# Splitting the first layer's filter copies by rounds, and drawing out the other layers' copies, in a four-layer convolution kernel

## The chip, the core and the metric

The kernel runs on one core of a Trainium2 chip. A core has five engines with queues of their own: TensorE (PE, with its weight loads PEld), VectorE (DVE), ScalarE (ACT), GpSimd (POOL) and SyncE (SP), which in this kernel issues the DMAs. Sixteen DMA engines move the data. The metric is the device time of one execution in microseconds (us); several executions are made and their median is taken.

## The reference

Four layers work on x of shape (4, 64, 256, 256), that is batch, channel, row, column. Layers 0, 2 and 3 are long two-dimensional convolutions, each with its own weights; layer 1 works in Haar space.

```python
h = sin(freq * (z @ w1 + b1)); h = sin(freq * (h @ w2 + b2)); h = sin(freq * (h @ w3 + b3))
h = (h @ wo) * exp(-t * abs(deltas))          # once for X, once for Y: hx, hy
k = einsum('ijk,imk->ijmk', hx, hy)           # a filter per channel, an outer product
y = irfft2(rfft2(x) * rfft2(k) / fft_size)[..., :L, :L]
out = y + x * bias                            # layers 0, 2, 3

f1 = haar2d(x)                                # layer 1
for i in range(2):
    f4 = einsum('bchw,oc->bohw', f1 * v[i], conv_w[i])
    acc += sign(f4) * relu(abs(f4) - tau[i])
out = haar2d(acc, inverse=True) + x
```

The filter of a channel is an outer product of two causal filters of 256 taps, so a convolution layer is two products with triangular Toeplitz matrices, one along each image axis. The small network that makes the taps is the same function for the three convolution layers ("first": layer 0; "other layers": 2 and 3, which the kernel counts as 1 and 2).

## The kernel before

The work is cut into three phases. Phase A does layer 0 and the forward Haar transform, phase B the channel mixing of layer 1, phase C the inverse Haar transform and layers 2 and 3. The images are two groups of two, and a round is two channels of one group: 32 rounds a group, 64 in phase A.

**A round of phase A** is ten pieces (`A_PIECES`), functions called one after another; `piece(t, j)` is piece j of round t, at place 10t + j. In pieces 0 to 3 TensorE multiplies round t's rows by the first Toeplitz blocks (`rows`, tile a1ps); in pieces 4 and 5 it does the Haar product of round t-3 (`product`, a3ps); in pieces 6 to 9 it does the columns of round t-1 (`columns`, a2ps). ACT copies a1ps out (L444), DVE adds the residual (`residual`, L464) and scales a3ps (L477), POOL does the rest of the Haar transform of round t-2 (L344, L346). The copies and residuals of a piece are issued at the start of the next piece (`later`, `flush`). All DMAs of the phase are issued by SP, in the order of the program: `filters(t + 2)` in piece 2 (two loads of overlapping rows from DRAM, L158), `store(t - 3)` in piece 7 (coef, L481), `load(t + 2)` in piece 9 (x, four loads in the first group, L147). The x tiles are three, so a load waits until the last residual that reads its buffer is done.

**The filters.** `network(ls)` gives a list of small functions for the networks of layers `ls`: for each of three depths a product on TensorE (L193, L195), a shift and six steps of a range reduction on DVE (L200 to L215), and a sine on ACT (L219); at the end, for each layer, three output products (L236), each with a multiplication by the decay on DVE (L241). The result stands in a tile `padded` of 64 rows (partitions): two for each round, each with three items of 320 elements. A Toeplitz load reads 64 shifted rows, so the taps have to stand repeated in DRAM, 20 times (`REPEATS`), in `filt`. `spread(l, begin, end, parts)` (L258) writes these repetitions for the rounds `begin` to `end`, as `parts` DMAs: each takes the partitions 2 begin to 2 end, reads them with a step of 0 over its share of the 20 repetitions, and writes 3840 bytes for each row and repetition (L264). The filters of the first four rounds (`FIRST`) are made in another way, by a product that gives the repetitions at once (`repeated`, L227), before phase A begins.

The copies of the remaining 28 rounds of layer 0 are `spread(0, FIRST, ROUNDS, BLOCKS)`: four DMAs of 56 rows by 5 repetitions, issued in pieces 0 to 3 of round 0.

**What is set beside phase A.** The list `rest` (L282 to L285) holds a load of weights for the other layers (`wbd`), the 39 functions of `network([1, 2])` and the 20 copies of the two other layers, ten each, of 64 rows by 2 repetitions: 60 entries. `beside(main, side, lead, tail)` (L949) calls the pieces of `main` and after each as many entries of `side` as keep the two lists in step, spread evenly from piece `lead` to `tail` pieces before the end. The call `beside(a[:cut_a], rest, 2, 3 * A_PIECES)` has 348 pieces with 2 and 30 left out, so 60 entries over 316 pieces: one in every 5.27. After `cut_a`, in round 34, the network's tiles are given back and phase B begins beside the second group's rounds.

The pieces' part that the change touches:

```python
            if t == 0 and j < BLOCKS:
                copies[j]()
            if j == 2:
                filters(t + 2)
...
        copies = spread(0, FIRST, ROUNDS, BLOCKS)
```

## Time and profile before

| What | Before |
|---|---|
| Median of 3 runs | 2587.52 us (2584.11 to 2591.82) |
| The profiled execution | 2585.35 us, span 2583.6 us |
| Mean granted TensorE clock | 0.977 |
| Busy: TensorE, weight loads | 2319.3 us (90%), 1848.1 us (72%) |
| Busy: VectorE, ScalarE, GpSimd | 1823.0 us (71%), 1324.7 us (51%), 2064.4 us (80%) |
| DMA | 685.23 MB, mean 265 GB/s |
| `filt` copies of layer 0 | 4 of 1050 KB, issued from 26.6 to 35.1 us |
| `filt` copies of the other layers | 20 of 480 KB, issued from 274.5 to 387.5 us |
| `toep` loads, whole kernel | 384 of 224 KB, median 5.3 us from issue to landing |

The span runs from the first to the last instruction; the execution's time has a little around it. Shares of busy time are means over phases of different kinds. Phase A alone runs from about 24 us to 425 us, and from there beside phase B. The profile can also be asked for a window, for one engine's instructions in order of time, or for one engine's waits; a line such as "x<-in_x x4" is four instructions in a row that write tile x from the input of that name, with the start of the first and the time of all. "SPq" is the issuing of DMAs, which says nothing of how long their data take. A bracket behind an instruction gives the idle time of its engine before it and what ended that.

### The profile page before, as it was taken

The page shows a single profiled execution, that of the slowest core. Times are in us where ns is not written, and L with a number is a line of the kernel's source. Part 1 is how long each engine was busy: PE and PEld are TensorE (multiplying, and loading weights), DVE is VectorE, ACT ScalarE, POOL GpSimd, SP SyncE. Part 2 cuts the span into 40 slices and gives each one's busy share as a digit, 9 for nine tenths or more (in the row PEclk, how much of TensorE's full clock was granted, in tenths as well). Part 3 has the DMA queues.
Part 4 walks back from the last instruction along what each step waited for, and adds up shares of the span by engine and source line. Part 5 has one row for each costly group of instructions (what it writes and reads, how often), then busy time and mean ns, then how long its engine had stood idle before and what let it go on. Part 6 is the DMA issues. An engine that isn't in the chain of part 4 may idle for free.

```text
span 2583.6 us, 118458 instructions
## 1 busy us (share of the span) xinstructions
PE 2319.3 (90%) x53292; PEld 1848.1 (72%) x53292; DVE 1823.0 (71%) x2049; ACT 1324.7 (51%) x2187; POOL 2064.4 (80%) x2428
## 2 busy tenths in 40 slices
PE   5999999678888888757999999999989999999999
PEld 4877877444444444546777778777789998999998
DVE  2555445799999999646677777766757777777763
ACT  1221212566666666325666666666655655655552
POOL 1898887899989999767676777766779999999991
PEclk8999999899999999978999999999999999999999
DMA  7676998699999999555988999988876666666653
GB/s 210 216 244 234 298 309 283 243 342 323 337 340 316 351 321 330 182 194 194 331 301 309 317 320 323 313 306 297 288 233 211 223 213 212 221 216 208 219 166 111
DMA packets 203676, 685.23 MB, mean 265 GB/s; under 512 B 29289, under 2 KB 30826, under 8 KB 190755
## 3 DMA queue, kind: packets, MB, share of 16 engines
q1 hardware_dynamic: 203171, 677.67, 77.1%
q8 instruction: 418, 6.85, 1.1%
q14 instruction: 87, 0.71, 0.1%
HBM read 427.93 MB, written 249.63 MB: 262 GB/s over the span
## 4 chain that ended last, share of the span: by engine, by line
PE 60%; DVE 14%; POOL 10%; DMA 6%; issue 5%; ACT 3%; SPq 2%; DVEq 0%; ACTq 0%; POOLq 0%
PE c2c L296 11%; PE c2r L296 10%; PE c1r L296 9%; PE c1c L296 9%; PE a1ps L296 6%; PE a2ps L296 6%; PE f L607 4%; PE c0ps L308 4%; POOL fw L344 3%; DVE m L651 3%; POOL f L346 3%; DVE x L626 3%; DVE a L646 2%; PE a3ps L308 2%; DVE x L464 2%
## 5 line engine op out<-in xcount | busy, mean ns | idle before, releaser
L385 POOL TENSOR_TENSOR i<-i,g 128x16 f32<-128x16 f32 x744 | 431.5, 601 | 27.7 <-ACT g L362 0.6
L296 PEld LDWEIGHTS a2ps<-toep,ay 64*64 64x64 f32 x8192 | 305.5, 137 | 163.9 <-DVE f L477 86.4
L296 PE MATMUL a2ps<-toep,ay 64*64 64x128 f32 (+3 forms) x8192 | 357.7, 306 | 47.9 <-DVE f L477 42.3
L607 PE MATMUL f<-ft,mix 64*64 64x512 f32 x2048 | 297.3, 617 | 111.6 <-DVE x L626 94.3
L296 PEld LDWEIGHTS a1ps<-toep,x 64*64 64x64 f32 x8192 | 288.4, 134 | 89.7 <-issue 45.4
L296 PE MATMUL a1ps<-toep,x 64*64 64x64 f32 (+3 forms) x8192 | 337.6, 300 | 16.6 <-DMA x<-in_x 11.4
L296 PEld LDWEIGHTS c2c<-toep,ch 64*64 64x64 f32 x8192 | 300.0, 135 | 58.9 <-issue 19.1
L296 PE MATMUL c1r<-toep,z 64*64 64x192 f32 (+3 forms) x8192 | 319.0, 300 | 22.6 <-issue 11.9
L296 PEld LDWEIGHTS c1c<-toep,ch 64*64 64x64 f32 x8192 | 296.2, 134 | 57.8 <-issue 18.5
L296 PEld LDWEIGHTS c1r<-toep,z 64*64 64x64 f32 x8192 | 292.4, 135 | 59.2 <-issue 28.0
L296 PE MATMUL c2c<-toep,ch 64*64 64x256 f32 (+3 forms) x8192 | 314.7, 299 | 8.4 <-ACT ch L848 6.8
L296 PE MATMUL c1c<-toep,ch 64*64 64x128 f32 (+3 forms) x8192 | 310.3, 298 | 9.0 <-ACT ch L848 5.5
L669 POOL TENSOR_TENSOR gt<-m,ft 128x512 f32<-128x512 f32 x128 | 163.5, 1277 | 193.7 <-DVE m L651 188.8
L385 POOL TENSOR_TENSOR ci<-i,g 128x1024 f32<-128x1024 f32 x124 | 313.9, 2552 | 4.5
L444 ACT COPY ay<-a1ps 128x512 f32<-128x512 f32 x256 | 137.4, 589 | 351.2 <-PE a1ps L296 350.6
L296 PEld LDWEIGHTS c2r<-toep,cy 64*64 64x64 f32 x8192 | 287.9, 134 | 32.9 <-issue 15.2
L632 ACT ACTIVATE m<-x 128x1024 f32<-128x1024 f32 x194 | 206.1, 1062 | 205.3 <-DVE x L626 98.5
L296 PE MATMUL c2r<-toep,cy 64*64 64x192 f32 (+3 forms) x8192 | 310.1, 297 | 1.3 <-issue 1.1
L848 ACT COPY ch<-c2r 128x512 f32<-128x512 f32 x256 | 137.3, 591 | 280.2 <-PE c2r L296 279.5
L477 DVE TENSOR_TENSOR f<-a3ps,wrow_sb 128x512 f32<-128x512 f32 x256 | 161.3, 683 | 130.2 <-PE a3ps L308 130.2
L626 DVE TENSOR_TENSOR x<-f,v 128x1024 f32<-128x1024 f32 x192 | 233.5, 1216 | 22.1 <-PE f L607 20.5
L344 POOL TENSOR_TENSOR fw<-x 128x1024 f32<-128x1024 f32 x64 | 122.2, 1910 | 150.4 <-DVE x L464 137.9
(83 smaller groups left out, 3976.8 us busy)
## 6 DMA issues: line engine op xcount, KB each, us to landing
toep<-filt SPq DMA_DIRECT2D x384, 224.0 KB, 5.3
ft<-coef SPq DMA_DIRECT2D x128, 512.0 KB, 7.6
v<-in_v SPq DMA_DIRECT2D x64, 1024.0 KB, 10.1
mixed<-gt SPq DMA_DIRECT2D x128, 512.0 KB, 7.2
g<-mixed SPq DMA_DIRECT2D x256, 256.0 KB, 5.1
x<-in_x SPq DMA_DIRECT2D x128, 256.0 KB, 4.4
coef<-f SPq DMA_DIRECT2D x128, 256.0 KB, 4.0
x<-in_x SPq DMA_DIRECT2D x32, 1024.0 KB, 8.0
```

What stands on the lines that cost most here:

```text
L296: nc.tensor.matmul(ps[r][half(c), j % 2, k * ROW :], data[half(r), c, k, bass.ts(j, ROW)], t(r, c)[:, : N - k * ROW], start=k == 0, stop=k ...
L308: nc.tensor.matmul(ps[r][half(c)].rearrange("p h k -> p (h k)"), matrix[half(r)], pairs(r, c).rearrange("p h k -> p (h k)"), start=True, s ...
L344: nc.gpsimd.tensor_tensor(diffs, even, odd, ALU.subtract)
L346: nc.gpsimd.tensor_tensor(sums, even, odd, ALU.add)
L385: engine.tensor_tensor(to, s, d, op)
L444: later(lambda y=y, ps=ps: nc.scalar.copy(y, ps))
L477: later(lambda f=f, ps=ps, w=w: nc.vector.tensor_tensor(f, ps, w, ALU.mult))
L607: nc.tensor.matmul(un[u]["f4"][half(q), b, :], mixers[0][half(r), bass.ts(i, C)], st[s]["f"][half(r), b], start=True, stop=True, tile_posi ...
L626: nc.vector.tensor_tensor(un[u]["x"], un[u]["f4"], both(u, "v"), ALU.mult)
L632: nc.scalar.activation(un[u]["m"], un[u]["x"], AF.Sign)
L669: nc.gpsimd.tensor_tensor(g[:, 0], m[:, 0], st[s]["f"][:, 0], ALU.add)
L848: later(lambda y=y, ps=ps: nc.scalar.copy(y, ps))
```

## The change

The four copies of layer 0 become seven, one for every four rounds (`CHUNK`), each with all 20 repetitions of 8 rows, 600 KB. The dictionary `copies` says in which round one is issued: the one for rounds 4 to 7 in round 0, the one for 8 to 11 in round 2, and so on every fourth round (6, 10, 14, 18, 22), six rounds ahead of its first use, always in piece 1, ahead of the Toeplitz load in piece 2.

The list `rest` is drawn out with empty entries: one ahead of each function of the networks, and nine ahead of each copy (`APART` - 1). It has 1 + 78 + 200 = 279 entries over the same 316 pieces, one in 1.13. So a network function comes in every 2.27 pieces, from round 0 to round 9, where it came in every 5.27, from round 1 to round 21; and a copy of the other layers comes in every 11.3 pieces, from round 10 to round 31, where it came in every 5.27, from round 21 to round 31. Data, sizes of the other layers' copies and all arithmetic stay as they are.

```diff
 FIRST = 4
+CHUNK = 4
+APART = 10
...
     rest = []
     rest.append(lambda: wbd_sb.extend(constant(f"wbd{l}", wbd[:, l], [P, 2, P]) for l in (1, 2)))
-    rest += network([1, 2])
-    rest += spread(1, 0, ROUNDS, 10) + spread(2, 0, ROUNDS, 10)
+    for p in network([1, 2]):
+        rest += [lambda: None, p]
+    for copy in spread(1, 0, ROUNDS, 10) + spread(2, 0, ROUNDS, 10):
+        rest += [lambda: None] * (APART - 1) + [copy]
...
-            if t == 0 and j < BLOCKS:
-                copies[j]()
+            if j == 1 and t in copies:
+                copies[t]()
...
-        copies = spread(0, FIRST, ROUNDS, BLOCKS)
+        copies = {max(0, t - 6): spread(0, t, t + CHUNK, 1)[0] for t in range(FIRST, ROUNDS, CHUNK)}
```

## The prediction

> **What bounds the kernel now.** I read the table of busy time by stage first, because the page's averages hide where the edit acts. Its columns are the stage, each engine's busy time, the granted TensorE clock, the DMA share and GB/s.

> ```profile
> core 0: us, PE busy (x) PEld busy (x) DVE busy (x) ACT busy (x) POOL busy (x), PEclk, DMA share, GB/s
> 0.00:40.00 40.00, 23.79 (x348) 15.98 (x349) 13.55 (x33) 6.83 (x12) 1.47 (x8) 1.00 0.74 199
> 40.00:80.00 40.00, 26.96 (x583) 25.12 (x586) 10.43 (x18) 4.30 (x8) 17.87 (x25) 0.79 0.66 191
> 120.00:160.00 40.00, 40.00 (x1044) 31.85 (x1040) 23.84 (x37) 8.05 (x15) 36.19 (x63) 1.00 0.69 233
> 280.00:320.00 40.00, 39.85 (x1031) 32.72 (x1027) 21.19 (x32) 7.24 (x15) 35.78 (x64) 1.00 0.97 317
> 360.00:400.00 40.00, 36.20 (x920) 30.66 (x915) 18.46 (x29) 6.44 (x12) 30.34 (x55) 1.00 0.91 298
> ```

> From 80 to 310 us TensorE is full and the DMA engines are idle a quarter of the time. It has holes at the start (0 to 80) and once the DMA share is above 0.9. Next the chain of waits (start, duration, what):

> ```profile
> 123.38 4.37 PE a1ps L296 x128
> 133.83 4.37 PE a1ps L296 x128
> ...
> 306.66 4.42 PE a1ps L296 x109
> 339.43 4.78 PE a1ps L296 x90
> 389.76 4.52 PE a1ps L296 x115
> ```

> The first two lines are one full round, 10.45 us. Round 25 starts at 306.66, round 28 at 339.43, round 32 at 389.76: from 28 to 32 a round takes 12.6 us. From round 24 (first matmul at 296.03) to round 34 (411.40), ten rounds take 115.4 us where full ones take 104.5: 10.9 us lost. Then SP's queue, start and duration of issue:

> ```profile
> 24.61 1.87 SPq L147 DMA_DIRECT2D x<-in_x  x4
> 26.58 3.13 SPq L264 DMA_DIRECT2D filt<-padded  x3
> 29.76 5.29 SPq L158 DMA_DIRECT2D toep<-filt  x2
> 35.09 2.59 SPq L264 DMA_DIRECT2D filt<-padded  x1
> 37.72 5.55 SPq L169 DMA_DIRECT2D wbd_sb<-in_wbd  x2
> 43.32 8.38 SPq L147 DMA_DIRECT2D x<-in_x  x4
> ...
> 81.77 2.50 SPq L147 DMA_DIRECT2D x<-in_x  x4
> 84.78 1.20 SPq L158 DMA_DIRECT2D toep<-filt  x2
> 86.88 3.64 SPq L481 DMA_DIRECT2D coef<-f  x4
> ```

> and TensorE's own timeline:

> ```profile
> 42.87 4.07 PE L296 MATMUL a2ps<-toep,ay 64*64 64x256 f32 x60 [3.22 <-issue]
> 56.57 1.08 PE L296 MATMUL a1ps<-toep,x 64*64 64x256 f32 x2 [9.63 <-DMA x<-in_x]
> 58.19 7.18 PE L296 MATMUL a1ps<-toep,x 64*64 64x256 f32 x118 [0.54 <-DMA x<-in_x]
> ```

> The four first-filter copies hold back the load of x_2, and round 2 waits for it until 58. In a full round (79.92) the x load for the next one goes out 1.85 us in, when the residual frees its buffer, the Toeplitz load at 4.9, the store at 7.

> [...] each 56-row copy (partitions 8 to 63) landed in 14 single increments, each 64-row copy in 16. [...] a 3840-byte packet of the 64-row copies takes 149 ns alone and 293 ns in the crowd[...]. The coef stores, 64 rows too but every second partition, take 159 ns for 4096 bytes on the same 16 engines, so the halving belongs to partitions, not to engines. [...] x_2, issued behind the copies, came when they had landed (34.98, 40.94, 47.06, 53.27: 6.1 us each). [...] Above, 118 matmuls took 7.18 us after a 9.63 us hole; 128 take 4.37 in a full round.

> **The change part by part.**

> *The first filters' copies.* Four DMAs of 56 rows x 5 repeats become seven of 8 rows x 20 repeats, 614 KB each, in piece 1 of rounds 0, 2, 6, 10, 14, 18, 22. The bytes are the same (4.3 MB). [...] By the two-engine figure a packet is 2 x 293 = 586 ns, so 20 take 11.7 us (estimate[...]). The seven take 82 us against 24.5 now, on engines that carry everything else.

> Startup: x_1 has left the engines at 29.4, where the first copy packet starts now. The copy ends at 41.1; the Toeplitz load adds 1.5, the wbd weights (256 KB) 0.7, x_2 3.3, the landing 1.2: 47.8 against 58.2. Of these 10 us I keep 9 at round 4, since the second copy (begun about 53, ended 65) leaves x_4 behind it: 65 + 1.5 + 2.7 + 1.2 = 70.4 against 79.9 now. **9 us won.**

> The copy of round 6, in a full stage, round start T. SP passes x_7 at T+1.85 to 4.3, then the copy, two Toeplitz loads, four coef stores, and x_8's four parts from T+12.3. Engines 0 to 7: x_7 done at 5.5, copy until 17.2, Toeplitz 1.5 (18.7), coef 2.8 (21.5), x_8 3.3 (24.8), landing 1.2: T+26. SP also cycles through eight DMA semaphores in the trace, and x_8's second part is the eighth DMA behind the copy, so it is not issued before about T+18. TensorE wants x_8 at T+20.9[...]: 5 us of stall, and about 1 for the half clock. **6 us lost.** Queued behind the waiting matmul are all later rounds, so ACT's copies, DVE's residuals and POOL's transform shift with it.[...]

> Copies of rounds 10, 14, 18, 22 meet the other layers' copies (below). A round costs each engine 7.9 us of packets, a 64-row copy 1.66 us, now every 1.13 rounds: 9.4. Four rounds with a first-filter copy ask 4 x 9.4 + 11.7 = 49.3 us of engines 0 to 7, and have 41.8. The missing 7.5, with imperfect packing (the 12.6 us rounds are 0.93 busy), is 8 us a copy, from 7 to 11. **32 us lost.** The extra SP issues (three DMAs, 0.4 to 0.6 us each) lie in SP's idle time.

> *The other layers' copies.* Twenty 480 KB copies at pieces 217 to 317 (1.9 a round) move to 102 to 317 (0.88 a round). Rounds 24 to 33 then need 9.4 us of DMA in 10.45, and the stage at 285 to 306 kept full rounds with 9.95. So the 10.9 us go, less a little. **10.5 us won.**

> *The networks.* The 39 pieces go from a-pieces 12 to 212 to 5 to 91. TensorE's share is the same: two products lengthened rounds 5 and 10 by 1.4 and 1.2 us, six outputs rounds 15 to 20 by 0.7 each; 7 us, paid in either place, or up to 2 hidden in stalls. DVE's 13 us (for each of three depths two shifts of 0.5, three steps of 0.42 and three of 0.7) fall on nine rounds in place of twenty: DVE goes from 6.2 us of 10.45 (23.84 of 40 above) to about 7. A sine stands 2.3 pieces behind its last DVE step, so ACT's row copies behind it could wait 1 us, three times. I take 0 (-2 to +3). The wbd loads pass x_2's by no more than now. POOL gets nothing.

> Sum: -9 + 6 + 32 - 10.5 = +18.5. The profiled execution took 2585.35 us (span 2583.6 and 1.75 around it), 2.2 under the median of 2587.52. So 2604 by it, 2606 by the median; I give 2605. Phase B starts behind round 34 and shifts one to one.

> **Rivals.**

> *The narrow copies cost nothing* (the rival on the other side: [...]the idle quarter of the DMA time swallows the copy; it decides from a copy that holds engines 0 to 7 for less than about 4 us, with a price of 3). Then x_2 lands near 29.4 + 3 + 6.7 = 39, and round 2 starts where round 1 ends, at 46.9[...]: 58.2 - 46.9 = 11.3 plus some 3.5 of half clock, 15 us won, plus 10.5: 2560. For it: full rounds at a DMA share of 0.97. Against: 293 ns beside 149, and an x load with only about 2.5 us to spare (issued 81.8 to 84.3, median 4.1 to landing, wanted at 90.4).

> *The losses balance the gains.* The copies stall 4 us each in place of 8: -9 + 4 + 16 - 10.5 = 0.5, about 2587. For it: the 1.9 copies a round begin in round 21 and the first long round is 26, so some backlog is carried without a stall.

> [...]

> **How the numbers follow.** Forecast 0.62 (own range 2593 to 2622); free 0.20; balance 0.12[...]. A measurement here can tell 0.3%, 7.8 us. Slower by more: 0.62 + 0.06 = 0.68; same 0.12; faster 0.20. The range 2562 to 2625 leaves out half of the free case[...] and the forecast's tail.

> **What would show it.** Right: waits of TensorE for x<-in_x two rounds behind rounds 6, 10, 14, 18 and 22, of 4 to 11 us; landings of the new copies near 12 us and 3840-byte packets near 586 ns; rounds 27 to 33 at 10.45; round 3 starting near 57 to 60. Wrong: copies landing in 3 to 6 us, or full rounds through 10 to 26; then the time is near 2560.

## The result, and the profile after

The changed kernel takes 2604.05 us (median of 6 runs, 2598.79 to 2609.45) against 2583.36 us before (6 runs, 2579.76 to 2591.82): ratio 1.0077, 95% interval 1.0056 to 1.0098. It is slower by 20.7 us; the prediction said 2605, 18.5 us slower. The profiled execution took 2599.17 us with a span of 2597.4, which is 13.8 us more than the profiled span before, so it lies at the fast end of its kernel's runs. The engines' work is what it was (the matmul count is the same, 53292); the time went into holes of TensorE and into stretches behind them at half clock (a granted clock of 0.50 in the trace).

The table of busy time by stage of the kernel after, with the columns shown for before:

```profile
0.00:40.00 40.00, 25.27 (x408) 17.41 (x408) 17.08 (x39) 6.83 (x12) 1.47 (x8) 1.00 0.61 160
40.00:80.00 40.00, 35.16 (x792) 28.26 (x796) 20.71 (x30) 7.50 (x14) 28.72 (x42) 0.91 0.76 228
160.00:200.00 40.00, 37.31 (x911) 31.32 (x914) 17.29 (x26) 6.44 (x12) 29.57 (x53) 0.96 0.92 301
240.00:280.00 40.00, 34.34 (x825) 30.21 (x821) 15.91 (x25) 6.44 (x12) 28.82 (x51) 0.91 0.84 249
360.00:400.00 40.00, 40.00 (x1043) 37.89 (x1038) 19.64 (x30) 8.59 (x16) 35.46 (x62) 1.00 0.87 300
```

TensorE does 8 us more in 40 to 80 than before, and 360 to 400 is full again. In exchange the middle (160 to 320), full before, has lost 3 to 7 us in 40. A narrower window just behind the copies of rounds 6 and 14 tells what the DMA engines did there:

```profile
95.00:108.00 13.00, 13.00 (x308) 9.31 (x300) 6.90 (x11) 3.37 (x7) 12.38 (x19) 1.00 0.67 143
193.00:206.00 13.00, 10.83 (x290) 9.19 (x281) 5.29 (x8) 2.59 (x5) 11.92 (x19) 1.00 0.67 140
```

and a window of the same length in the kernel before:

```profile
134.00:147.00 13.00, 13.00 (x352) 10.41 (x347) 7.79 (x12) 2.60 (x5) 12.21 (x24) 1.00 0.68 228
```

The DMA share is the same, 0.67 and 0.68, but 140 GB/s move in place of 228: a packet counts as busy for as long as it takes, and the packets of the new copies take longer (a median of 573 ns for 3840 bytes, where the other layers' copies of 64 rows mostly show 149 or 293). SP's queue of the kernel after, around the copy of round 14 (start, duration of issue):

```profile
193.53 0.76 SPq L266 DMA_DIRECT2D filt<-padded  x1
194.39 5.89 SPq L160 DMA_DIRECT2D toep<-filt  x2
200.38 7.68 SPq L485 DMA_DIRECT2D coef<-f  x4
208.10 1.13 SPq L266 DMA_DIRECT2D filt<-padded  x1
209.33 3.82 SPq L149 DMA_DIRECT2D x<-in_x  x4
```

Behind the copy at 193.53 two Toeplitz loads take 5.9 us to issue, where they took 1.2, and four stores 7.7 where they took 3.6: SP is held back (the profile does not say by what), and x_16 goes out only at 209.33. Each of the seven copies landed in eight single increments, 14.1 to 15.4 us after its issue. Where no other copy runs beside it, seven or eight of its 160 packets are under way at once for 64 to 82% of its length, so it is called here a copy on eight engines, with 20 packets for each. Which engines they are no record says: "engines 0 to 7" is the prediction's name for them. The chain of waits near the end of the first group has its full rounds back:

```profile
362.37 4.37 PE a1ps L300 x112
372.84 4.36 PE a1ps L300 x114
```

From one to the next is a full round of 10.47 us, where the kernel before took 12.6. TensorE's timeline behind the copies of rounds 10 and 14 is a surprise:

```profile
162.11 5.38 PE L300 MATMUL a2ps<-toep,ay 64*64 64x128 f32 x105 [3.70 <-issue]
210.47 2.50 PE L300 MATMUL a1ps<-toep,x 64*64 64x64 f32 x33 [6.64 <-issue]
```

In the second line TensorE has stopped for 6.64 us in the middle of a round's rows; "issue" says that the profile shows nothing that it waits for, and x_15, which it is multiplying, had landed at 197.9. All of TensorE's own waits from 80 to 340 us in the kernel after (total, times, longest):

```profile
PE a1ps L300 <- issue: 17.0, 4, 6.6
PE a2ps L300 <- issue: 3.9, 2, 3.7
PE a1ps L300 <- DMA x<-in_x: 3.0, 4, 1.3
```

So 21 us of the holes end with no data arriving, and only 3 us with an x load. Another 15.4 us, in four stretches at the ends of the four long stops, TensorE worked at half clock (granted 0.50), where the clock before stood at 1.00 from 64 to 345 us; by the prediction's two figures, 7.18 us for 118 matmuls there (granted 0.61 over that time) and 4.37 for 128 in a full round, that costs some 7 us (an estimate).

The trace also records packets that bring instructions, 16384 bytes each, among the packets of the DMA engines. From 80 to 330 us one starts every 5.0 us (median), but not behind the copies: from 148.7 the next is 11.1 us later, from 194.6 13.4, from 243.7 12.0, from 297.9 9.9. That TensorE runs out of instructions there became the rival to test.

Counting settles much of it. The span has 418 of these packets and 107204 recorded instructions of TensorE (matmuls, weight loads and what its sequencer does), about 256 for each packet, so the packets are TensorE's. And at each of the four long stops the number of instructions that it had started is exactly 449 plus 256 for each packet that had ended by then (22, 30, 38 and 47 packets); it goes on 1.4 to 1.6 us after the next packet has ended. The two waits for x_8, at 114 and 116 us, do not stand at such places: 15 packets had ended, and TensorE had more than 180 of their instructions left. The reserve is small: when one of these packets starts, TensorE has, in 19 of 20 cases, at most 253 delivered instructions left, and a full round uses 544 in 10.45 us, so that is under 5 us of work (an estimate).

### The profile page after: what moved, and what is told of

It is laid out like the page before. It is cut to its first block, busy times and chain, and to the rows that moved or that the text cites. A ratio compares the mean times of both kernels' runs of the same rounds, so it can differ in the third digit from the quotient of the medians.

```text
span 2597.4 us, 118459 instructions
## 1 busy us (share of the span) xinstructions
PE 2330.5 (90%) x53292; PEld 1880.0 (72%) x53292; DVE 1828.5 (70%) x2049; ACT 1324.5 (51%) x2187; POOL 2064.2 (79%) x2428
## 4 chain that ended last, share of the span: by engine, by line
PE 59%; DVE 15%; POOL 8%; DMA 7%; issue 5%; ACT 4%; SPq 2%; DVEq 0%; ACTq 0%; POOLq 0%
PE c2c L300 10%; PE c2r L300 10%; PE c1r L300 9%; PE c1c L300 9%; PE a1ps L300 6%; PE a2ps L300 5%; PE f L611 4%; PE c0ps L312 4%; DMA v<-in_v 4%; DVE m L655 3%; DVE x L630 3%; POOL fw L348 2%; POOL f L350 2%; DVE a L650 2%; PE a3ps L312 2%
## 5 line engine op out<-in xcount | busy, mean ns | idle before, releaser
L300 PEld LDWEIGHTS a2ps<-toep,ay 64*64 64x64 f32 x8192 | 313.6, 138 | 154.8 <-DVE f L481 85.2
L300 PE MATMUL a1ps<-toep,x 64*64 64x128 f32 (+3 forms) x8192 | 345.0, 303 | 26.0 <-issue 17.2
L300 PEld LDWEIGHTS a1ps<-toep,x 64*64 64x64 f32 x8192 | 296.7, 136 | 98.2 <-issue 52.9
L300 PE MATMUL c1r<-toep,z 64*64 64x128 f32 (+3 forms) x8192 | 313.0, 299 | 17.5 <-ACT z L840 10.3
L300 PE MATMUL c2c<-toep,ch 64*64 64x128 f32 (+3 forms) x8192 | 309.1, 299 | 7.9 <-ACT ch L852 5.4
L300 PE MATMUL c1c<-toep,ch 64*64 64x64 f32 (+3 forms) x8192 | 308.4, 299 | 8.4 <-ACT ch L852 5.6
L300 PEld LDWEIGHTS c2r<-toep,cy 64*64 64x64 f32 x8192 | 290.6, 134 | 34.1 <-issue 21.5
L300 PE MATMUL c2r<-toep,cy 64*64 64x128 f32 (+3 forms) x8192 | 309.3, 298 | 6.3 <-issue 5.9
L481 DVE TENSOR_TENSOR f<-a3ps,wrow_sb 128x512 f32<-128x512 f32 x256 | 161.2, 683 | 147.7 <-PE a3ps L312 146.3
```

The costliest lines, as they stand in the source:

```text
L300: nc.tensor.matmul(ps[r][half(c), j % 2, k * ROW :], data[half(r), c, k, bass.ts(j, ROW)], t(r, c)[:, : N - k * ROW], start=k == 0, stop=k ...
L481: later(lambda f=f, ps=ps, w=w: nc.vector.tensor_tensor(f, ps, w, ALU.mult))
```

## The experiments

All times are compared with the kernel before on the same chip. The first two diffs are against the kernel before, the others against the changed kernel, unless another is named; only the lines that matter are shown. A profiled execution of one kernel can lie 11 us from its median, so the table after the experiments counts the delay round by round instead.

**One part alone.** First the drawn-out list without the new copies:

```diff
-    rest += network([1, 2])
-    rest += spread(1, 0, ROUNDS, 10) + spread(2, 0, ROUNDS, 10)
+    for p in network([1, 2]):
+        rest += [lambda: None, p]
+    for copy in spread(1, 0, ROUNDS, 10) + spread(2, 0, ROUNDS, 10):
+        rest += [lambda: None] * (APART - 1) + [copy]
```

> The kernel before with the drawn-out list alone (networks in every second piece, the other layers' copies one a round); the four 56-row copies of layer 0 stay in round 0. Theory (narrow reads: the loss is all in the 8-row copies, the drawn-out copies are a clean gain): the ten rounds 24 to 33 fall from 115 us to about 105, nothing is lost before, so about 10 us faster than before, 2574. Rival (the networks in nine rounds and the copies from round 10 cost as much as they bring): within 3 us of before.

Measured: 2576.35 us against 2583.5, ratio 0.9977 (0.9962 to 0.9991). Two of its stages, same columns:

```profile
280.00:320.00 40.00, 39.67 (x1057) 36.76 (x1052) 20.06 (x31) 7.51 (x14) 36.09 (x64) 1.00 0.86 282
360.00:400.00 40.00, 40.00 (x1042) 35.26 (x1037) 20.01 (x31) 8.59 (x16) 36.52 (x61) 1.00 0.84 282
```

The stages that had holes at a DMA share of 0.91 and more are full, at 0.84 to 0.86. The list is a gain by itself, 7 us by the medians where 10 were expected; the interval reaches from 2 to 10. Then the new copies without the list:

```diff
-            if t == 0 and j < BLOCKS:
-                copies[j]()
+            if j == 1 and t in copies:
+                copies[t]()
...
-        copies = spread(0, FIRST, ROUNDS, BLOCKS)
+        copies = {max(0, t - 6): spread(0, t, t + CHUNK, 1)[0] for t in range(FIRST, ROUNDS, CHUNK)}
```

> The kernel before with the seven 8-row copies alone; networks and the other layers' copies stay as before. Theory (narrow reads): start won by 11 us, then about 7 us lost behind each of the copies of rounds 6, 10, 14, 18 although no other copies run there, and 7 or more at round 22: 2583 - 11 + 35 = 2607. Rival (loss only where both kinds of copies meet): 7 us at round 6 and 7 at round 22 at most, 2583 - 11 + 14 = 2586 or less.

Measured: 2614.65 us, ratio 1.0115 (1.0098 to 1.0131), nearly 8 us over what was expected. The copies do harm alone: about 5 us behind each of the copies of rounds 10, 14 and 18, with no other copies near. TensorE's waits from 80 to 340 us here:

```profile
PE a1ps L298 <- DMA x<-in_x: 10.3, 7, 2.4
PE a1ps L298 <- DVE x L466: 3.7, 3, 1.5
PE a2ps L298 <- issue: 2.3, 1, 2.3
```

In this kernel it is mostly the x load that comes late, as predicted. Both sorts of wait occur, then.

**The rows apart.** The rows of the filter tile are put in another order, so that the eight rows of a copy stand four partitions apart. The columns of the network's last weights and of the decay are put in that order (`placed`), and the loads of the other layers find their rows in it; nothing else changes:

```diff
+def _place(row):
+    return 32 * (row // 32) + 4 * (row % 8) + row % 32 // 8
...
-            start = filt[l].offset + (t % ROUNDS * 2 + r) * REPEATS * SPAN
+            row = t % ROUNDS * 2 + r
+            start = filt[l].offset + (_place(row) if l else row) * REPEATS * SPAN
...
-            src = filters[l][at].rearrange("p k e -> p (k e)").unsqueeze(1)
+            p = _place(2 * begin)
+            of = at if l else slice(p, p + 29, 4)
+            src = filters[l][of].rearrange("p k e -> p (k e)").unsqueeze(1)
...
-        "wo": f(np.stack([w[:, filters.T] for w in wo], axis=1)),
-        "decay": f(_decay()[filters]),
+        "wo": f(np.stack([w[:, placed.T] for w in wo], axis=1)),
+        "decay": f(_decay()[placed]),
```

> The changed kernel, with the rows of the filter tile put in another order: the eight rows of a copy stand in every fourth partition (4h + c), not in eight neighbours. Same DMAs, same bytes, same places in SP's order, still eight engines. Theory[...]: [...]packets fall from 573 ns to about 149, a copy lands in 4 to 5 us, the stalls behind rounds 6 to 22 go (some 36 us less): about 2604 - 36 = 2568, 15 us under before. Rival ([...]a row read 20 times is slow): packets stay above 450 ns and the time at 2600 or more.

Measured: 2556.34 us, ratio 0.9901 (0.9874 to 0.9928), 27 us faster than before, where 15 were expected. The packets of the copies fall to a median of 149 ns, the copies land in 6.3 to 8.5 us. Its second stage, and a window behind its copy of round 6:

```profile
40.00:80.00 40.00, 40.00 (x993) 31.94 (x994) 27.25 (x39) 9.65 (x18) 35.64 (x52) 1.00 0.67 221
...
87.00:100.00 13.00, 13.00 (x304) 9.35 (x300) 6.89 (x11) 3.29 (x7) 12.37 (x19) 1.00 0.91 317
```

317 GB/s in place of 143 with the same seven DMAs of eight rows, and TensorE is full from 40 to 80 us. So in this kernel a copy of eight rows alone does little harm (149 ns a packet, 2556 us); with its rows in two groups of four neighbouring partitions it does (573 ns, 2604 us). A step between comes from every second partition, so four groups of four with two rows in each (diff against the version just shown):

```diff
-    return 32 * (row // 32) + 4 * (row % 8) + row % 32 // 8
+    return 16 * (row // 16) + 2 * (row % 8) + row % 16 // 8
...
-            of = at if l else slice(p, p + 29, 4)
+            of = at if l else slice(p, p + 15, 2)
```

> The changed kernel with the eight rows of a copy in every second partition, so over four groups of four and two engines on each. Theory[...]: packets near 293 ns, 20 of them 5.9 us, landing 8 to 10 us; little stall is left, 2556 to 2568, and not under the version with every fourth partition. Rival (it is neighbouring partitions as such, not the groups of four): packets near 149 ns or near 573 ns.

Measured: 2567.67 us, ratio 0.9937 (0.9913 to 0.9960); landings 8.6 to 9.6 us. The packets of its copies are of two sorts, most near 149 and near 293 ns (median 229 before 138 us). So in these copies of eight rows a packet took 149 ns with one row in a group of four partitions, near 149 or near 293 with two, and 573 with four, which is 2.0 and 3.8 times 149. What makes the packets of neighbouring rows slow each other is not shown beyond these times. Little stall is left: 3.7 us of waits of TensorE from 80 to 340 us.

**What the wait is.** From round 3 to 31 the x loads go into a tile that nothing reads, and TensorE multiplies the tile of round 2 instead. What this kernel leaves out is the use of those images, so its output is another:

```diff
-        xs = big("in", f"x_{t}", 3)
+        xs = spare if 2 < t < ROUNDS else big("in", f"x_{t}", 3)
...
+                if t == 2:
+                    kept.append(st[t]["x"])
+                if 2 < t < ROUNDS:
+                    st[t]["x"] = kept[0]
```

> The changed kernel, with x loaded from round 3 to 31 into a tile that nothing reads, while TensorE and the residuals read the tile of round 2 (so layer 0 is computed from the wrong images in the first group; DMA traffic is the same, but no product waits for an x load). Theory as predicted (x arrives late behind the copy): the stalls behind the copies of rounds 6 to 22 go, 2604 - 36 = 2568. Rival (TensorE's own instruction packets[...] are held up: the profile after shows gaps of 3.7 and 6.6 us that no x load ended): stalls of 4 to 7 us stay behind most of the five copies, 2590 or more.

Measured: 2598.16 us, ratio 1.0056 (1.0037 to 1.0076). TensorE's waits from 80 to 340 us:

```profile
PE a2ps L302 <- issue: 16.0, 2, 9.5
PE a1ps L302 <- issue: 7.0, 1, 7.0
PE a1ps L302 <- DMA toep<-filt: 1.6, 2, 1.1
```

With no x load to wait for, TensorE still stops for 6.5, 7.0 and 9.5 us behind the copies of rounds 6, 10 and 14. In the same places the instruction packets are 14.2, 13.2 and 15.8 us apart, and each of the three stops again stands at exactly 449 plus a multiple of 256 instructions (12, 21 and 29 packets), and ends 1.4 to 1.5 us after the next packet has ended. Behind the copies of rounds 18 and 22 no packet comes more than 7.8 us after the last, and there TensorE hardly stops. The rival is right: x late is one way to lose the time, instructions late the other, and taking the first away alone brought some 6 us (2598 for 2604). How a copy on eight engines holds an instruction packet up is not shown, since the records don't say on which DMA engine a packet ran. In the changed kernel the four late packets started between 0.1 and 5.1 us before the copy ahead of them had landed.

**Burst or amount.** Each copy is cut into four DMAs of five repetitions, one in each of four rounds (two in each of rounds 0 and 1 for the first):

```diff
+            if j == 1:
+                for put in copies.get(t, []):
+                    put()
...
-        copies = {max(0, t - 6): spread(0, t, t + CHUNK, 1)[0] for t in range(FIRST, ROUNDS, CHUNK)}
+        copies = {}
+        for first in range(FIRST, ROUNDS, CHUNK):
+            for k, put in enumerate(spread(0, first, first + CHUNK, BLOCKS)):
+                copies.setdefault(k // 2 if first == FIRST else first - 6 + k, []).append(put)
```

> The changed kernel, with each of the seven copies cut into four DMAs of 8 neighbouring rows by 5 repetitions, one in each of four rounds in a row (two and two in rounds 0 and 1 for the first). [...]a single DMA holds its engines for 5 x 573 ns = 2.9 us. Theory A (throughput: engines 0 to 7 have 9.4 + 2.9 = 12.3 us of work in a round of 10.45 from round 10 to 25): rounds 2 to 9 full, then about 30 us lost as in the changed kernel; 2583 - 14 + 30 - 10 = 2589 or more. Theory B (burst: an x load or an instruction packet stands 12 us behind one copy): short holds do no harm, 2583 - 14 - 10 = 2560 to 2566.

Measured: 2570.53 us, ratio 0.9942 (0.9923 to 0.9961), between the two but much nearer to B. The same bytes leave the same two groups of four partitions, over four rounds in place of one, and the loss is mostly gone. The packets changed with it: before 138 us their median is 154 ns in place of 573, and 20 of them take an engine 5.6 us in place of 9.5 (means). Half of them ran at 149 ns, like the packets of the rows apart; why is not shown. So this run shortens the burst and the engines' total time at once, and does not tell the two apart.

**Both together, and the list undone.** The rows apart with the other layers' list as before (the removed lines of the first diff put back):

> The seven copies with their rows in every fourth partition, and the list of the other layers as in the kernel before. Theory (parts add up): the start's 18 us stay won, rounds 24 to 33 cost their 10 us again: 2556 + 8 to 10 = 2565. Rival (the drawn-out list and the narrow copies only help one another): 2575 or more.

Measured: 2566.7 us, ratio 0.9939 (0.9915 to 0.9962). That is the 2565 expected: the parts add up. And the rows apart with the copies in quarters (the diffs of the rows apart and the burst experiment together):

> Both mendings together: rows of a copy in every fourth partition, and each copy cut into four DMAs of 5 repetitions in rounds in a row. Theory (what harms is how long one copy holds its engines): a part holds them for 5 x 149 ns = 0.75 us against 3.4 in the version with every fourth partition alone; the few us that this one loses in rounds 11 to 16 go, 2550 to 2558, not to be told from 2556. Rival (20 more DMAs on SP cost issue time and semaphores): 2565 or more.

Measured: 2558.51 us, ratio 0.9906 (0.9884 to 0.9928): not to be told from the rows apart alone (2556.34), and so no sign that the quarters bring more. Its TensorE has one sort of wait left from 80 to 340 us:

```profile
PE a1ps L303 <- issue: 1.9, 3, 1.3
```

**The delay by rounds.** The end of the last residual of a round on DVE, less that of the kernel before, in us, from each profiled execution (negative is earlier):

| Kernel | round 1 | 5 | 9 | 13 | 17 | 21 | 23 | 33 |
|---|---|---|---|---|---|---|---|---|
| after | -11.4 | -10.8 | -4.5 | 2.8 | 8.7 | 16.9 | 23.9 | 13.9 |
| list alone | -1.6 | -0.9 | 1.5 | 2.7 | -0.2 | -1.7 | -1.7 | -12.0 |
| copies alone | -12.9 | -11.0 | -7.7 | -2.6 | 2.7 | 8.0 | 17.6 | 17.5 |
| rows apart | -19.3 | -18.7 | -16.2 | -13.3 | -16.0 | -16.1 | -15.9 | -23.8 |
| x unread | -11.9 | 2.9 | 7.9 | 27.9 | 25.8 | 25.3 | 27.8 | 17.7 |
| quarters | -17.9 | -17.3 | -14.8 | -12.3 | -14.1 | -10.0 | -10.0 | -16.7 |
| every second | -18.2 | -17.5 | -15.1 | -12.7 | -14.2 | -13.5 | -12.4 | -19.0 |
| apart, old list | -19.7 | -19.7 | -19.7 | -19.7 | -19.5 | -19.5 | -19.0 | -18.4 |
| apart, quarters | -19.4 | -18.8 | -16.3 | -16.0 | -17.8 | -18.9 | -18.9 | -26.5 |

The networks stand in different rounds in the two lists, which bends the rows with the new list by up to 4 us in rounds 5 to 17 and is gone by round 21 (second line). What is there in round 33 stays to the end: the kernel after is 13.0 us behind in round 63 too.

## Why the prediction was right, and where its steps were not

*The cost of a narrow copy* (586 ns a packet, 11.7 us): right, 573 ns and eight single increments. That the 293 ns of the copies before would double was the author's estimate; the versions with one and two rows in a group have the 149 and 293 ns. The landing, 14.1 to 15.4 us after the issue, came later than the 12 given as a sign.

*The start, 9 us won*: 11.4 in round 1, of which the list has 1.6. TensorE's timeline after:

```profile
43.78 0.96 PE L300 MATMUL a1ps<-toep,x 64*64 64x256 f32 x2 [3.82 <-DMA x<-in_x]
45.80 7.03 PE L300 MATMUL a1ps<-toep,x 64*64 64x256 f32 x126 [1.07 <-DMA x<-in_x]
```

x_2 came near 46, not 47.8. The late x_4 that was to keep back part of the gain at round 4 wasn't there: the second copy was issued at 45.8, where the prediction had it begin near 53, and had landed at 59.9, so x_4 passed and round 4 began at 68.7 in place of 70.4.

*The copy of round 6, 6 us lost*: 6.3 from round 5 to 9, of which the networks' shift is 2.4 (second line of the table), so 3.9 where 6 were given. x_8 landed at 118.15, and 2.7 us of wait for it stand in the timeline: the mechanism as given, and a third of the size not there.

*The copies of rounds 10 to 22, 32 us lost*: 28.4 from round 9 to 23, where the list alone wins 3.2, so 31.6. The number is right, and its reason is the step that failed, in two ways. First, the loss was worked out as an amount: 49.3 us of work for a copy's eight engines in rounds that give 41.8. The kernel with the copies alone speaks against that. Behind its copies of rounds 10, 14 and 18 no other copies run; by the prediction's 7.9 us a round and the measured packet, four rounds there ask 4 x 7.9 + 11.5 = 43.1 us, 1.3 more than there are (with the 7.3 us a round that the packets before take from 80 to 270 us, nothing is missing), and 5.1 to 5.3 us were lost behind each. What costs, as these runs read, is the time for which one DMA is under way, 14 to 15 us from issue to landing: behind it, in the changed kernel, the instruction packets come 10 to 13 us apart in place of 5.0. (The quarters fit this, but with their 5.6 us the amount, too, gives a small loss, 4 x 9.4 + 5.6 = 43.2 against 41.8.) Second, the wait at the end was to be x: behind these four copies it was mostly TensorE's own instructions, 20.4 us of stops, a transfer that the prediction had not in its account at all. That the sum fits is in this part luck: two accounts of one blockage came to the same size.

*The other layers' copies, 10.5 us won*: 10.0 after round 23 in the changed kernel, 10.3 in the list alone. ("Idle a quarter" up to 310 us holds only until the first of these copies, at 274; the prediction's own line for 280 to 320 has a share of 0.97.) The prediction took the long rounds before for a lack of DMA time. The share is high (0.91 and more), but here too what TensorE stops for is instructions. One of four such stops, from the kernel before:

```profile
357.44 0.66 PE L296 MATMUL a1ps<-toep,x 64*64 64x192 f32 x13 [1.66 <-issue]
```

The four, near 344, 356, 368 and 386 us, make 5.9 of the 10.9 us, and all stand at exactly 449 plus a multiple of 256 instructions.

*The networks, 0*: -1.7 by round 21, and -1.6 of it stands in round 1 already, so by then the functions themselves have cost nothing.

*The rivals.* "The narrow copies cost nothing" was not this kernel, but it is what the kernel becomes once the rows stand apart: 2560 was worked out for it, 2556 and 2558 were measured. The balance, and a copy of 23 us (the 0.06 in the prediction's sum), are ruled out by the 573 ns, which make 11.5 us for 20 packets, and by the time.

*The sum.* The parts as measured come to 13.9 us in round 33 of the profiled execution, where 18.5 were added up; the medians differ by 20.7. That 2605 and 2604.05 lie so close is partly chance: the prediction started from 2585 to 2587 us, and the six runs of the kernel before have their median at 2583.36.

## What to carry to other kernels

A DMA's price is not its bytes alone: look at how many partitions it reads and how they lie. In this kernel, giving the eight rows of one transfer to different groups of four partitions was worth some 48 us against the changed kernel (2604 to 2556). Where a DMA share stays the same while GB/s fall by more than a third, look at the time of single packets; here packets of an eight-row copy took 573 ns from two groups of four neighbouring partitions and 149 from eight groups, and behind such copies x loads came late and TensorE's instruction packets up to 13.4 us apart. The one transfer that had to be slow here did less harm in four parts, spread out, than in one.
